# Softmax reciprocals in three bfloat16 parts, and counts as bfloat16 matmuls, in an attention and mixture-of-experts kernel

## The chip, the cores and the metric

The kernel runs on one core of one Trainium2 chip. A core has five engines with a queue of instructions each: TensorE (PE in the profile, with its weight loads as PEld), VectorE (DVE), ScalarE (ACT), GpSimd (POOL), and SyncE (SP), which here only issues DMA transfers. Every queue is worked off in order. The metric is the device time in microseconds of one execution.

## The reference, cut to what matters

One layer: attention with a gated relative position bias, a layer norm, a top-2 mixture of 8 experts with a capacity per expert, and a second layer norm. The input has 8 batches of 1024 tokens of width 256; there are 16 heads of width 16.

```python
scores = jnp.einsum('bhid,bhjd->bhij', q, k) * scale + gated_bias
attn = jax.nn.softmax(scores, axis=-1)
out = jnp.einsum('bhij,bhjd->bhid', attn, v)
...
x = _layernorm(x + out.transpose(0, 2, 1, 3).reshape(B, N, E) @ Wo.T + bo)
...
for e in range(E):                      # the experts, in order
    match = topk_experts == e
    elig = match.any(-1) & ~fallback
    pos = jnp.cumsum(elig) - 1          # a token's place in the expert's buffer
    kept = elig & (pos < cap)
    overflow = elig & (pos >= cap)
    ...
    fallback = fallback | overflow
```

Two things in it matter here: the softmax's division by a sum per row and head, and the running count of tokens per expert (`cumsum`), from which each token's place follows.

## The kernel before, in words

The kernel has two halves. In the first, attention runs and the tokens are sorted by expert into a DRAM buffer `xd`; in the second the experts run over that buffer. The change touches only the first half.

**Units and steps.** The first half is a loop over 64 *units* (8 batches by 8 pairs of heads, `HP = 2`), each of 16 *steps*: 8 blocks of 128 keys (`j`) by 2 chunks of 512 queries (`c`). The loop variable is `g`; `u, s = divmod(g, STEPS)`. The scheduler is switched off here: each engine gets its instructions in the order in which this loop calls the helpers. A step does this:

- `scores` (L1107): two bfloat16 matmuls into the PSUM tile `sc`; `exps` (L1120): DVE adds the gated bias `gb` near the diagonal, ACT writes `pr = exp(sc)`.
- `products` (L1137), in each odd step: `v` times `pr` into the PSUM tile `o_acc`, for four pairs of head and chunk at partitions 0, 32, 64 and 96. `v` has a 17th column of ones, so row `r + D` of each group of 32 holds the sums of the softmax.
- `max_first`, `max_second`, `max_fold`: 21 steps ahead of it (`LEAD`), the row maxima for a later unit: four matmuls into `pm` (L1028, L1032), a relu on ACT into `over` (L1057), a fold on DVE (L1069). `shift` (from step 11) turns the maxima of a unit into two rows of `qs`.
- POOL makes `gb` two blocks ahead (`gate_biases`, L988) and the diagonal matrices `dgb` (L1001).
- SP issues the loads for later units in fixed steps: `biasb` (step 1), `ks` and its differences (3 and 4), `qs` (6), two halves of `gates` (8 and 15), `bias` (0).

**The division, before.** At the end of step 1 of unit u+1, `take_outputs(u)` (L1151) lets ACT copy `o_acc` to `osb`. What follows is put into a list of deferred calls by `after(n, what)`; `tick`, once in a step, counts down and calls what is due. One step on, four DMAs spread the four rows of 512 sums over 128 partitions by 16 columns (`move_sums`, L1159). Two steps after that DVE takes the reciprocal (L1175), one step later four DMAs bring them back as four rows of 512, `recs` (L1169). In step `DIVIDE_AT = 10`, `divide` (L1178) is queued: a float32 matmul of the 4x128 matrix `sel` with `recs` spreads each row over 32 partitions (`pb`, L1182), DVE multiplies `osb` by it (L1186), and four DMAs store the result into `oD` (L1196). `osb` has one buffer, so the next unit's copy of `o_acc` waits for these stores.

**The shared bank.** One PSUM bank (`bank(name)`) serves all side work: the projections of the next batch (`prologue`), the output projection, the router and the counting of the batch before (`epilogue`), the shift and the division. `Streams` hands it out. A side task is a generator that yields what it needs: BANK (a matmul into the bank comes next), HELD or SLOW (the bank is read in the next step, by ACT or by DVE), FREE or ODD. While a task holds the bank nobody else gets it. `streams.own` has the shift and the division, which come first:

```python
if u and s == DIVIDE_AT:
    streams.own.append(divide(u - 1))
if s == SHIFT_AT and u + 1 < UNITS:        # SHIFT_AT = 11
    streams.own.append(shift(u + 1))
behind = c == 0 and streams.read == SLOW
others = s + 1 != SHIFT_AT
if not behind:
    streams.bank(others)
```

**The counts, before.** In the epilogue, for each of the eight experts and the fallback, POOL makes running sums within a partition (`running`, L812; its operations all carry the line L754) into `prefix` and `incl`. `count` (L822) then makes two float32 matmuls with constant 128x128 matrices: `ones` against the batch's running sums (L824), and `later` against the batch's own marks (L825), both into `pc`. DVE reads `pc` and gives the place and the spill, from which POOL goes on with the next expert. In the last batch these nine counts run after the loop, with nothing beside them. The epilogue then starts `scatters`, which sends one indirect store from POOL (L891) in each odd step.

Of the kernel before, what the change touches and what calls it, by code (L numbers as in the profile page):

```python
# [11 lines left out]
F32 = mybir.dt.float32  # L12
BF16 = mybir.dt.bfloat16
# [3 lines left out]
ALU = mybir.AluOpType  # L17
# [4 lines left out]
P = 128  # L22
H, D = 16, 16
NG, HG = 4, 4
E = H * D
NE, TOP_K = 8, 2
FF = 1024
NBUCKET, MAX_DIST = 80, 200
CH = 512
# [14 lines left out]
HP = 2  # L44
LEAD = 21
SHIFT_AT = -LEAD % 16
DIVIDE_AT = 10
EPS = 1e-5


# [28 lines left out]
def tile_attention_moe(  # L79
# [25 lines left out]
    nc = tc.nc  # L105
    B, N, _ = x.shape
    T = B * N
    NI = N // P
# [44 lines left out]
    with ExitStack() as at:  # L153
        cst = at.enter_context(tc.tile_pool(name="cst", bufs=1))
# [3 lines left out]
        rt = at.enter_context(tc.tile_pool(name="rt", bufs=1))  # L158
# [24 lines left out]
        def load_piece(b, n, tag="xp", bufs=3):  # L183
# [21 lines left out]
            out=gb_ld.rearrange("p g o -> p (g o)"), in_=gru_b.to_broadcast([P, 8])  # L205
# [59 lines left out]
        for base, sign in ((0, 1), (D - 1, -1)):  # L265
# [17 lines left out]
            out=later, in_=later, compare_op=ALU.is_gt, fill=0.0, base=0,  # L283
            pattern=[[-1, P]], channel_multiplier=1,
        )
        sel = cst.tile([4, 4, 32], F32, name="sel")
        nc.gpsimd.memset(sel, 0.0)
        nc.gpsimd.affine_select(
            out=sel, in_=sel, compare_op=ALU.not_equal, fill=1.0, base=0,
            pattern=[[-1, 4], [0, 32]], channel_multiplier=1,  # L290
        )
        rank = cst.tile([P, NE], F32, name="rank")
        nc.gpsimd.iota(
            rank, pattern=[[-1, NE]], base=NE, channel_multiplier=0,
# [27 lines left out]
        for lo, hi in zip(cuts[:-1], cuts[1:]):  # L322
# [9 lines left out]
            out=blocks,  # L332
# [48 lines left out]
        for h in range(HP):  # L381
# [2 lines left out]
                nc.sync.dma_start(out=pattern[r : r + NI, h, :], in_=kcr[:NI, :])  # L384
            for r in range(R_SHIFT, R_ALL):
                nc.sync.dma_start(out=pattern[r : r + 1, h, :], in_=kcr[8:9, :])
        incl = [cst.tile([P, NE + 1, NI], F32, name=f"incl{i}") for i in range(2)]
        prefix = [cst.tile([P, 2 * NI], F32, name=f"prefix{i}") for i in range(3)]
        for t in prefix:
            nc.vector.memset(t, 0.0)  # L390
        o_acc = ps_o.tile([P, CH], F32, name="o_acc")
# [55 lines left out]
        def after(n, what):  # L447

            waiting.append([n, what])
# [230 lines left out]
        def epilogue(b, me):  # L680
# [140 lines left out]

            def count(e):  # L822
                pc = bank("pc")[:, :NI]
                nc.tensor.matmul(pc, ones, now[:, e, :], start=True, stop=False)  # L824
                nc.tensor.matmul(pc, later, who, start=False, stop=True)  # L825
                return pc

            spill = small("spill", NI)
# [26 lines left out]
            if b == B - 1:  # L855
                yield BANK
                pf = bank("pf")[:, : NE + 1]
                nc.tensor.matmul(pf, ones, now[:, :, NI - 1], start=True, stop=True)
                yield SLOW
                nc.vector.tensor_copy(counts, pf)  # L860
            ts = slice(b * NI, (b + 1) * NI)
# [289 lines left out]
        def take_outputs(u):  # L1151
            me = units[u]
            me.osb = work.tile([P, CH], F32, tag="osb", name=f"osb{u}", bufs=1)
            nc.scalar.copy(me.osb, o_acc)

            def move_sums():
                me.sums = rt.tile([P, 4 * CH // P], F32, tag="sums", name=f"sums{u}")
                for r in range(4):
                    nc.sync.dma_start(  # L1159
                        out=me.sums[r * 32 : (r + 1) * 32, :],  # L1160
                        in_=me.osb[r * 32 + D : r * 32 + D + 1, :].rearrange(
                            "o (p n) -> o p n", p=32
                        ),
                    )

            def move_back():
                me.recs = rt.tile([4, CH], F32, tag="recs", name=f"recs{u}")
                for r in range(4):
                    nc.sync.dma_start(  # L1169
                        out=me.recs[r : r + 1, :].rearrange("o (p n) -> o p n", p=32),  # L1170
                        in_=me.sums[r * 32 : (r + 1) * 32, :],
                    )

            after(1, move_sums)
            after(3, lambda: nc.vector.reciprocal(me.sums, me.sums))  # L1175
            after(4, move_back)

        def divide(u):  # L1178
            b, hp = divmod(u, UB)
# [140 lines left out]
                yield FREE  # L1320
                yield from prologue(b + 1, pieces)

        for g in range(G + 12):
            u, s = divmod(g, STEPS)
            j, c = divmod(s, NCH)
            b, sb = divmod(g, UB * STEPS)
# [323 lines left out]
```

## Time and profile before

| what | value |
|---|---|
| median of 3 runs | 3645.89 us (3643.89 to 3651.33) |
| the profiled execution: time, span | 3639.7 us, 3638.0 us |
| granted TensorE clock, mean | 0.962 |
| PE, DVE, ACT, POOL busy | 90%, 53%, 56%, 61% of the span |
| relu of the maxima on ACT (L1057), 1024 times | 597 ns each |
| exp on ACT (L1134), 1024 times | 1024 ns each |
| gated bias on POOL (L988), 512 times | 2092 ns each in the mean |
| the divide's matmul (L1182), 128 records for 64 divides | 646 ns each |
| reciprocal on DVE (L1175), 128x16, 64 times | 244 ns each |
| DMA issues of sums and of recs on SP, 256 each | 0.58 and 0.59 us each (median) |

How to read it: the profile is one execution. Busy shares are averages over both halves. A float32 matmul shows as two records, a bfloat16 one as one record with its load. The span counts from the first to the last instruction, and the measured time has a little around it. An idle time ahead of an instruction is put down to what ended it, the *releaser*. The time of a transfer's issue is SP's own; the data land later.

### The profile page before, as it was taken

How to read it: one execution, taken by the hardware profiler on the slowest of the kernel's cores; microseconds unless marked ns; L12 is line 12 of the kernel's file. 1: busy time of each engine (PE TensorE's matmuls, PEld its weight loads, DVE VectorE, ACT ScalarE, POOL GpSimd, SP SyncE). 2: the span in 40 equal slices, each digit the busy share in tenths (PEclk: the TensorE clock that was granted, in tenths of full speed). 3: DMA queues.
4: the chain of work that ended last, by engine and by line, in shares of the span. 5: the costliest groups of instructions: out<-in, count | busy, mean ns of one | idle time of the engine just before them, and what ended most of it. 6: DMA issues, size and time to landing. Idle time of an engine off the chain costs nothing. (4 is left out here: it accounts for less than half of the span.)

```text
span 3638.0 us, 53431 instructions
## 1 busy us (share of the span) xinstructions
PE 3266.2 (90%) x16263; PEld 1651.2 (45%) x16263; DVE 1926.7 (53%) x5559; ACT 2043.5 (56%) x3084; POOL 2225.2 (61%) x2619
## 2 busy tenths in 40 slices
PE   4798999989999999999999999993399999999997
PEld 2332343334334334334334433332267677667776
DVE  2565656655765766665666576651134344444343
ACT  1676777767777777787777777771122222222222
POOL 3567667776886887787797688782233333333332
PEclk7998999999999999999999999995699999999999
DMA  6567766656643453444444444320332332232220
GB/s 167 150 177 190 190 169 179 198 164 179 190 138 112 145 157 113 135 141 128 143 124 137 126 139 141 116 95 14 113 84 58 88 89 67 88 94 88 72 91 21
DMA packets 380417, 455.70 MB, mean 125 GB/s; under 512 B 87477, under 2 KB 285234, under 8 KB 380106
## 3 DMA queue, kind: packets, MB, share of 16 engines
q1 hardware_dynamic: 339146, 388.06, 36.2%
q0 software_dynamic: 19296, 43.38, 4.2%
q10 hardware_dynamic: 21664, 20.58, 1.8%
q8 instruction: 138, 2.26, 0.3%
q14 instruction: 173, 1.42, 0.1%
HBM read 315.16 MB, written 140.54 MB: 125 GB/s over the span
## 5 line engine op out<-in xcount | busy, mean ns | idle before, releaser
L1134 ACT ACTIVATE pr<-sc 128x1024 f32<-128x1024 f32 x1024 | 1047.6, 1024 | 316.4 <-DVE sc L1127 297.1
L988 POOL TENSOR_TENSOR gb<-bias,gates 128x1024 f32<-128x1024 f32 (+2 forms) x512 | 1070.9, 2092 | 132.4 <-DMA gates<-gd 80.2
L1069 DVE CUSTOM_DVE_ANT_0 over<-pm,over 128x512 f32<-128x512 f32 x1024 | 704.0, 688 | 816.4 <-ACT over L1057 301.1
L1057 ACT ACTIVATE over<-pm 128x512 f32<-128x512 f32 x1024 | 611.4, 597 | 276.0 <-PE pm L1032 259.4
L1112 PE MATMUL sc<-qs,ks 122*128 122x512 bf16 x2048 | 618.6, 383 | 32.5 <-ACT pr L1134 19.3
L1127 DVE TENSOR_TENSOR sc<-sc,gb 128x640 f32<-128x640 f32 (+3 forms) x768 | 600.0, 781 | 79.9 <-POOL gb L988 62.6
L1032 PE MATMUL pm<-biasb,dgb 128*128 128x320 bf16 (+2 forms) x2048 | 578.5, 282 | 0.0
L1142 PE MATMUL o_acc<-pr,v 128*17 128x512 f32 x4096 | 553.9, 612 | 0.2 <-ACT pr L1134 0.2
L1488 PE MATMUL ph<-xsT,w 128*128 128x512 f32 (+1 forms) x1440 | 488.3, 497 | 13.0 <-ACT xsT L1428 12.1
L1503 PE MATMUL py<-w,hT 128*128 128x256 f32 x2208 | 485.0, 379 | 5.6 <-DVE ys L1510 5.6
L1503 PEld LDWEIGHTS py<-w,hT 128*128 128x128 f32 x2208 | 419.2, 190 | 74.3 <-issue 9.8
L1028 PEld LDWEIGHTS <-qs 120*128 120x128 bf16 x2048 | 207.2, 101 | 518.4 <-issue 349.2
L1028 PE MATMUL pm<-ks_d,qs 120*128 120x512 bf16 x1024 | 392.8, 384 | 54.5 <-DMA qs<-qd 27.4
L1028 PE MATMUL pm<-ks,qs 120*128 120x512 bf16 x1024 | 396.7, 387 | 44.6 <-DVE mh L1069 26.4
L1495 ACT ACTIVATE hT<-ph,b_sb 128x512 f32<-128x512 f32 (+1 forms) x360 | 211.6, 588 | 288.0 <-PE ph L1488 259.9
L1488 PEld LDWEIGHTS ph<-xsT,w 128*128 128x128 f32 x1440 | 270.5, 190 | 213.1 <-issue 169.2
L1428 ACT COPY xsT<-pt 128x512 f32<-128x512 f32 (+1 forms) x90 | 39.5, 489 | 567.5 <-PE pt L1425 472.6
L143 POOL TENSOR_TENSOR rs<-rstd,neghalf 128x1 f32<-128x1 f32 x138 | 78.4, 568 | 441.3 <-DVE rstd L141 440.9
L1032 PEld LDWEIGHTS <-dgb 128*128 128x128 bf16 x2048 | 201.7, 98 | 260.6 <-issue 147.4
L1001 POOL TENSOR_TENSOR dgb<-anti,grev 128x256 bf16<-128x256 f32 x512 | 314.5, 615 | 4.9
L1112 PEld LDWEIGHTS <-ks 122*128 122x128 bf16 x2048 | 198.0, 99 | 216.4 <-issue 67.7
L1523 POOL DMA_INDIRECT out_dram<-o,dst_i x138 | 145.4, 1054 | 154.3 <-DVE o L145 71.4
(184 smaller groups left out, 2840.9 us busy)
## 6 DMA issues: line engine op xcount, KB each, us to landing
gates<-gd SPq DMA_DIRECT2D x128, 704.0 KB
biasb<-stripb SPq DMA_DIRECT2D x128, 288.0 KB
bias<-blocks SPq DMA_DIRECT2D x64, 512.0 KB
xd<-zero SPq DMA_DIRECT2D x51, 522.0 KB
ks<-kd SPq DMA_DIRECT2D x384, 64.0 KB
qs<-qd SPq DMA_DIRECT2D x384, 64.0 KB
yd<-zero SPq DMA_DIRECT2D x40, 512.0 KB
w<-in_w_dram ACTq DMA_DIRECT2D x16, 1024.0 KB
```

Of the source, the lines that this page charges most:

```text
L988: nc.gpsimd.tensor_tensor(gb_[:, :, off : off + hi - lo], me.bias[:, :, off : off + hi - lo], gates[:, :, lo - at : hi - at], ALU.mult,)
L1001: nc.gpsimd.tensor_tensor(dg, anti.unsqueeze(1).to_broadcast([P, HP, P]), batches[b].grev[:, i, hp * HP : (hp + 1) * HP] .unsqueeze(2) .to ...
L1028: nc.tensor.matmul(pm, QS[u % 3][:R_SHIFT, h, i * P : (i + 1) * P], keys, start=True, stop=False)
L1032: nc.tensor.matmul(pm[:, lo:hi, :], dgb[m - h][:, h, :], me.biasb[:, at : at + (hi - lo) * P].rearrange("p (j n) -> p j n", n=P)[:, :, :HALF],
L1057: nc.scalar.activation(me.over, pm, AF.Relu)
L1069: nc.vector.tensor_tensor_reduce(out=me.over, in0=me.rest, in1=me.over, scale=1.0, scalar=-3.0e38, op0=ALU.add, op1=ALU.max, accum_out=me. ...
L1112: nc.tensor.matmul(me.sc[:, h, :], ks[:, h, j * P : (j + 1) * P], qs[:, h, c * CH : (c + 1) * CH], start=True, stop=True,)
L1127: nc.vector.tensor_tensor(sc[:, :, lo - c * CH : hi - c * CH], sc[:, :, lo - c * CH : hi - c * CH], me.gb[j][:, :, off : off + hi - lo], A ...
L1134: nc.scalar.activation(pr, sc, AF.Exp)
L1142: nc.tensor.matmul(o_acc[r : r + D + 1, :], batches[b].v[:, j, hp * HP + h, :], prs[c][:, h, :], start=(j == 0), stop=(j == NI - 1),)
L1488: nc.tensor.matmul(ph[:, :size], w1_sb[:, k, f * P : (f + 1) * P], xsT[:, k, :size], start=(k == 0), stop=(k == NK - 1),)
L1503: nc.tensor.matmul(py, hT[:, f, t * P : (t + 1) * P], w2_sb[:, f, :], start=(f == 0), stop=(f == NF - 1),)
```

## The change

The sums go to 96 partitions by 64 columns instead of 128 by 16. Three DMAs put the same 4 rows of 512 sums on partitions 32 to 63, 64 to 95 and 96 to 127 of one tile `sums`, whose first 32 partitions hold ones. DVE takes the reciprocal of the whole tile, in the same step as before. Then a float32 reciprocal is written as the sum of three bfloat16 numbers: ACT rounds all partitions to bfloat16 into `rp`, and POOL subtracts what was rounded from the partitions 64 up (`first`, step 5); ACT rounds what remains on these, and POOL leaves on the partitions 96 up what then remains (`others`, step 6). So `rp[32:64]`, `rp[64:96]` and `rp[96:]` are the first, second and third part. In step 9 one DMA brings the 96 partitions back as 12 rows of 512. The divide is queued in step 12 and multiplies them by a 12x128 matrix `sel` in bfloat16, which adds the three parts up.

The tiles of the counts and the two constant matrices become bfloat16; whole numbers up to 256 are exact in it, and the counts that enter the matmuls are at most 64.

```diff
-DIVIDE_AT = 10
+DIVIDE_AT = 12
...
-        sel = cst.tile([4, 4, 32], F32, name="sel")
+        sums = cst.tile([P, 4 * CH // 32], F32, name="sums")
+        nc.vector.memset(sums[:32], 1.0)
+        ones16 = cst.tile([P, P], BF16, name="ones16")
+        nc.gpsimd.tensor_copy(ones16, ones)
+        later16 = cst.tile([P, P], BF16, name="later16")
+        nc.gpsimd.tensor_copy(later16, later)
+        sel = cst.tile([12, 4, 32], BF16, name="sel")
         nc.gpsimd.memset(sel, 0.0)
-        nc.gpsimd.affine_select(
-            out=sel, in_=sel, compare_op=ALU.not_equal, fill=1.0, base=0,
-            pattern=[[-1, 4], [0, 32]], channel_multiplier=1,
-        )
+        for a in range(3):
+            nc.gpsimd.affine_select(
+                out=sel, in_=sel, compare_op=ALU.not_equal, fill=1.0, base=-4 * a,
+                pattern=[[-1, 4], [0, 32]], channel_multiplier=1,
+            )
...
-        incl = [cst.tile([P, NE + 1, NI], F32, name=f"incl{i}") for i in range(2)]
-        prefix = [cst.tile([P, 2 * NI], F32, name=f"prefix{i}") for i in range(3)]
+        incl = [cst.tile([P, NE + 1, NI], BF16, name=f"incl{i}") for i in range(2)]
+        prefix = [cst.tile([P, 2 * NI], BF16, name=f"prefix{i}") for i in range(3)]
...
-                nc.tensor.matmul(pc, ones, now[:, e, :], start=True, stop=False)
-                nc.tensor.matmul(pc, later, who, start=False, stop=True)
+                nc.tensor.matmul(pc, ones16, now[:, e, :], start=True, stop=False)
+                nc.tensor.matmul(pc, later16, who, start=False, stop=True)
...
             def move_sums():
-                me.sums = rt.tile([P, 4 * CH // P], F32, tag="sums", name=f"sums{u}")
-                for r in range(4):
+                for a in range(3):
                     nc.sync.dma_start(
-                        out=me.sums[r * 32 : (r + 1) * 32, :],
-                        in_=me.osb[r * 32 + D : r * 32 + D + 1, :].rearrange(
-                            "o (p n) -> o p n", p=32
-                        ),
+                        out=sums[(a + 1) * 32 : (a + 2) * 32, :],
+                        in_=me.osb[D::32, :].rearrange("r (p n) -> r p n", p=8),
                     )
+
+            def first():
+                me.rp = rt.tile([P, 4 * CH // 32], BF16, tag="rp", name=f"rp{u}")
+                nc.scalar.copy(me.rp, sums)
+                nc.gpsimd.tensor_tensor(sums[64:], sums[64:], me.rp[64:], ALU.subtract)
+
+            def others():
+                nc.scalar.copy(me.rp[64:], sums[64:])
+                nc.gpsimd.tensor_tensor(me.rp[96:], sums[96:], me.rp[96:], ALU.subtract)
 
             def move_back():
-                me.recs = rt.tile([4, CH], F32, tag="recs", name=f"recs{u}")
-                for r in range(4):
-                    nc.sync.dma_start(
-                        out=me.recs[r : r + 1, :].rearrange("o (p n) -> o p n", p=32),
-                        in_=me.sums[r * 32 : (r + 1) * 32, :],
-                    )
+                me.recs = rt.tile([12, CH], BF16, tag="recs", name=f"recs{u}")
+                nc.sync.dma_start(
+                    out=me.recs.rearrange("q (p n) -> q p n", p=8), in_=me.rp[32:]
+                )
 
             after(1, move_sums)
-            after(3, lambda: nc.vector.reciprocal(me.sums, me.sums))
-            after(4, move_back)
+            after(3, lambda: nc.vector.reciprocal(sums, sums))
+            after(4, first)
+            after(5, others)
+            after(8, move_back)
...
-        for g in range(G + 12):
+        for g in range(G + DIVIDE_AT + 2):
```

The matmul that counts the totals after the last batch (L858) takes `ones16` in the same way.

## The prediction

> **What bounds the kernel now.** I read the page's first two parts, then the busy time by stretch, the waits of PE, the groups by line and shape, and the timeline around one divide.
>
> ```profile
> PE 3266.2 (90%) x16263; PEld 1651.2 (45%) x16263; DVE 1926.7 (53%) x5559; ACT 2043.5 (56%) x3084; POOL 2225.2 (61%) x2619
> ...
> PE   4798999989999999999999999993399999999997
> ...
> PEclk7998999999999999999999999995699999999999
> ```
>
> PE is full in both halves except at the start and at the seam (slices 27 and 28), where it idles and its granted clock falls. The change lies wholly in the first half (attention, to about 2545 us). The second half is not touched. By stretch, columns as in the header:
>
> ```profile
> core 0: us, PE busy (x) PEld busy (x) DVE busy (x) ACT busy (x) POOL busy (x), PEclk, DMA share, GB/s
> 1584.10:1613.90 29.80, 28.52 (x165) 9.94 (x164) 20.08 (x47) 24.75 (x35) 27.03 (x25) 1.00 0.54 158
> 1107.40:1149.30 41.90, 37.77 (x207) 15.66 (x205) 23.93 (x54) 31.53 (x52) 30.98 (x34) 1.00 0.42 117
> ```
>
> The first is a bare unit of 16 steps, the second one that also carries projections. In both PE leads: 1.3 us of 29.8 idle, 4.1 of 41.9. ACT has 5.1 and 10.4 us to spare, POOL only 2.8 and 10.9. So what leaves PE shortens a unit, until POOL stands in the way. PE's own waits:
>
> ```profile
> PE pm L1028 <- DMA qs<-qd: 27.4, 16, 8.0
> PE pm L1028 <- DVE mh L1069: 26.4, 56, 1.7
> PE sc L1112 <- ACT pr L1134: 19.3, 22, 5.1
> ...
> PE pb L1182 <- DMA recs<-sums: 11.7, 4, 9.1
> ```
>
> The first is a queue effect; the timeline shows where it arises (start, duration, engine):
>
> ```profile
> 1009.46 2.44 SPq L1169 DMA_DIRECT2D recs<-sums  x4
> ...
> 1012.54 2.67 SPq L918 DMA_DIRECT2D qs<-qd  x6
> ...
> 1013.45 1.09 PE L1182 MATMUL pb<-recs,sel 4*128 4x512 f32 x2
> ...
> 1014.47 0.39 PE L1028 MATMUL pm<-ks,qs 120*128 120x512 bf16 x1
> ...
> 1017.26 0.38 PE L1028 MATMUL pm<-ks_d,qs 120*128 120x512 bf16 x1 [1.88 <-DMA qs<-qd]
> ```
>
> SP spends 2.44 us on issuing the four recs loads, then the six qs loads for the unit after next; PE needs those at step 11 and stands 1.88 us. And pb holds PE from 1013.45 to 1014.47, 1.02 us.
>
> **The change part by part.**
>
> *The divide's matmul.* The groups by line and shape (busy, mean ns, idle before):
>
> ```profile
> L1182 PE MATMUL pb<-recs,sel 4*128 4x512 f32 x128 | 72.5, 646 | 21.3 <-DMA recs<-sums 11.7 <-DVE dif L654 5.2 <-DVE mh L1069 3.1
> ...
> L825 PE MATMUL pc<-prefix,later 128*128 128x8 f32 x144 | 28.3, 269 | 0.0
> L824 PE MATMUL pc<-incl,ones 128*128 128x8 f32 x144 | 27.1, 260 | 29.0 <-POOL incl L754 29.0
> ...
> L1175 DVE RECIPROCAL sums<-sums 128x16 f32<-128x16 f32 x64 | 15.6, 244 | 12.8 <-DMA sums<-osb 12.6
> ```
>
> A float32 matmul is two records, so a divide costs 72.5/64 = 1.13 us of PE. With bfloat16 it is one record of 512 columns; the nearest row is the scores matmul sc (122x512 bf16, 383 ns mean). Twelve rows instead of four stream no longer. Gain 64 x (1.13 - 0.38) = 48 us, all on the engine that bounds. Slots in the timeline give about 50: 1.02 us against some 0.22 from one bfloat16 512-column matmul to the next.
>
> *The counts.* 72 counts of two float32 matmuls, each two loads (about 190 ns) and two records. Two counts stand in the timeline beside scores: from pc's first record to the next matmul 0.47 us (934.30 to 934.77) and 0.36 us (939.55 to 939.91). With bfloat16 two loads of 98 to 101 ns (rows L1032, L1028) and two short records remain. Bounds: 0.20 us per count if the loads are not hidden, 0.10 if they are. No 8-column bfloat16 row exists; I take 0.2, nearer the two loads. 63 counts x 0.22 = 14 us. The last nine run alone at the seam in a chain of 3.03 us each, of which PE holds 1.06 (2514.39 to the DVE's 2515.45); half of it saved gives 9 x 0.5 = 4 us. POOL's small operations take 200 ns in float32; output in bfloat16 is no dearer (L422, 128x512 to bf16, 1158 ns, against L675, to float32, 1181). Together 18 us.
>
> *SP's queue.* Before, eight issues per unit (4 sums, 4 recs, 0.58 us each in the table of tiles); after, three and one. The recs load also moves from step 5, ahead of qs<-qd, to step 9, behind it and the gates load. So qs<-qd goes out 0.6 + 2.44 = 3.0 us earlier. Of its 27.4 us of waits 8.0 belong to unit 0, which has no divide. The other 15 waits (19.4 us, 2.0 us at most) should go. What is late next is the second row of the waits (DVE's fold), so I count 15. The gates load also goes out earlier, which POOL waits for but PE does not.
>
> The moved recs load has its own deadline. By the order of instructions the divide does not run at step 12 but at 13: at step 12 the shift still holds the shared bank. From issue at 9 that is four steps, 7.5 us at 29.8/16 = 1.86 us each. Ahead of it lies the gates load, 704 KB, at 158 GB/s 4.6 us. The Trainium skill (DMA: Bandwidth & Descriptors, Queues, rings and completion order) says that an engine of the DMA consumes descriptors in ring order, which speaks against this place: 96 small packets wait for the whole 704 KB. With the rule recs land some 6 us after the gates issue, some 3 us ahead of the divide (gates is issued at step 8); if they overtook it, more. Neither makes PE wait, so nothing is charged; but a unit with other traffic could lose a microsecond.
>
> *Later stores.* The product on DVE moves from step 11 to 14, the four oD stores with it, and since they stand on SP ahead of gates, bias and biasb of the next unit, those slip by about 3 us (SP today waits 271.9 us for that product at L1196, so SP has the room). Then the next sums load queues behind 704 + 512 + 2 x 288 KB. In a bare unit the reciprocal, four steps into the next unit, may wait for it: 0 at best, 1 us in some 35 bare units at worst. DVE is 67% busy there and passes only part on to PE: I charge 10 us, and keep 0 to 35. osb itself is overwritten at the next unit's step 1, three steps after the stores: 5.6 us for 4 issues of 0.58 and the landing; tight but enough.
>
> *DVE.* The reciprocal grows from 16 to 64 columns. Rows: 203 ns at 8 columns (L768), 244 at 16, so 5.1 ns per column and 490 ns at 64. The Trainium skill (VectorE: DVE Perf Modes, First, the fixed hardware budget) gives an iterative divide with a repeat count of 8; eight cycles of its 0.96 GHz are 8.3 ns per column, estimated 644 ns. By the rows DVE gains 64 x 0.25 = 16 us of work, by the rule 26. I take the rows. It hides under DVE's third of idle time.
>
> *ACT and POOL.* Two copies on ACT per unit: 128x16 takes 173, 128x256 405, so 128x64 about 0.25 us, 32 us in all; ACT keeps over 4 us of room per bare unit. Two subtractions on POOL: 128x64 takes 321 ns (L754), so 0.64 us per unit, 41 in all. POOL has room except in the last and first unit of a batch, where each odd step also sends an indirect store of 1.01 us. There DVE waits for POOL today (62.6 us in 43 waits, DVE sc L1127 <- POOL gb L988), so 8 units pay 0.64: 5 us. Those units also don't cash the 1 us saved on PE: 8 us.
>
> The wait that is added: ACT's second copy (step 6) stands behind POOL's first subtraction (step 5), and behind ACT's copy stand relu and exp, for which PE waits. Where POOL is on time the chain is copy, subtract, copy inside one step. Where it lags, in those two units per batch, ACT can stand up to about 3 us: in the unit that starts at 1026.0 POOL ends step 5's dgb at 1047.1, ACT ends step 6's exp at about 1044.4. Mostly this takes the place of DVE's wait for gb further on; I charge 1 us in 8 units, 8 us; bounds 0 and 16 x 3 = 48.
>
> *The rest.* Three constants, two copies and two selects at the start, beside the first loads: nothing; if that cover were gone, 1 us. The tail trades four issues against two copies and two subtractions: 0, within 1.5 us either way.
>
> **The sum.** 48 + 18 + 15 - 10 - 5 - 8 - 8 = 50 us. It is made against the profiled execution, 3639.7 us (span 3638.0 and 1.7 around it), which gives 3590. The runs shown have their median 6 us above it, 3645.9; there the same gain gives 3596. I predict 3592 between them.
>
> **The rivals.**
> 1. *PE takes it all.* Slack hides every added piece, and the qs waits go entirely: 48 + 18 + 19 = 85, with 50 for the divide 87, about 3558. For it: PE leads in nearly every unit. Against: POOL's 2.8 us of room. Chance 0.25.
> 2. *POOL or ACT stands next.* The stalls at step 6 and the late sums cost their upper bounds in part, some 50 to 60 us instead of 31: gain 15 to 30, about 3622. For it: the 62.6 us that DVE waits for POOL today. Chance 0.18.
> 3. *Slower.* One place: the reciprocal behind the next unit's loads. If the ring is not drained by step 4, DVE, and behind it the fold and every score, stand in each unit. The gross gain of 81 is eaten from 1.3 us per unit (81/64); at 2 us per unit it costs 128 against 81 and the time is about 3690. For it: the loads slip by 3 us and DVE already waits for sums (12.6 us, six times). Against: units with projections are 36 to 46 us long and have room; only bare ones are tight. Chance 0.09.
> 4. *No change in sum*, within 0.2% (7 us, about what a measurement of this kernel can tell): 0.04, between 2 and 3.
> The forecast case, 3570 to 3610, has 0.44.
>
> The range: 3550 leaves out about half of rival 1's tail, 3635 takes in rival 2; some 0.2 lie outside. Faster: 0.44 + 0.25 + 0.18 = 0.87; same 0.04; slower 0.09.
>
> **What would show it.** Right: pb one record of about 0.38 us per divide and 25 us in all; PE pm <- qs<-qd down to unit 0's 8 us; the bare unit 28.5 to 29 us instead of 29.8; the second half unchanged. Wrong: a row of DVE sums <- DMA sums<-osb above 50 us (rival 3); a row of ACT's copy into rp waiting for POOL above 30 us (rival 2); PE pb <- DMA recs in many units (the moved load too late); ACT's copy of o_acc waiting for the oD stores.

## The result and the profile after

The changed kernel takes 3737.81 us (median of 4 runs, 3734.93 to 3739.59), against 3644.89 us of the kernel before (3638.43 to 3651.33): a ratio of 1.0254, 95% interval 1.0235 to 1.0274. It is 93 us slower; the forecast was 50 us faster.

The page of the profiled execution (span 3735.5 us):

```profile
PE 3258.7 (87%) x16054; PEld 1625.1 (44%) x16054; DVE 1948.7 (52%) x5560; ACT 2064.3 (55%) x3212; POOL 2259.9 (60%) x2751
...
PE   4898898889889889898988988985199999999998
...
PEclk7999899999999999999999999996599999999999
```

PE executes 209 records fewer (two of float32 became one in 64 divides, four became two in 72 counts, two one in the last count), yet its busy time falls by only 7.5 us, and 9s have become 8s over the whole first half. The mean granted clock is 0.949 instead of 0.962. The second half runs as before. From the first score matmul to the end of the last, before and then after (length, PE busy with its records, granted clock, DMA):

```profile
117.48:2456.03 2338.55, 2176.79 (x12001) 0.98 0.51 150
```

```profile
119.96:2552.15 2432.19, 2167.97 (x11811) 0.96 0.49 144
```

94 of the 97.5 us by which the two spans differ lie there. PE's busy time in these units fell by 9 us, and its idle time grew by 102.

The groups by line and shape (busy, mean ns, idle before) show that each changed operation has about the size that was forecast:

```profile
L1199 PE MATMUL pb<-recs,sel 12*128 12x512 bf16 x64 | 25.0, 391 | 17.9 <-DMA recs<-rp 17.8
L834 PE MATMUL pc<-incl,ones 128*128 128x8 bf16 x72 | 12.4, 173 | 75.5 <-POOL incl L764 67.8 <-DVE mh L1079 6.0
L1190 DVE RECIPROCAL sums<-sums 128x64 f32<-128x64 f32 x64 | 34.9, 545 | 40.3 <-DMA sums<-osb 40.2
L1177 POOL TENSOR_TENSOR sums<-sums,rp 64x64 f32<-64x64 f32 x64 | 19.4, 304 | 185.6 <-ACT rp L1176 102.8 <-ACT lg L755 19.9 <-DMA ks_d<-dd 14.4
L1180 ACT CAST rp<-sums 64x64 bf16<-64x64 f32 x64 | 15.4, 241 | 31.4 <-POOL sums L1177 30.1
```

What is not as forecast is the last column. POOL now stands 102.8 us for ACT's first copy, a wait that the kernel before does not have. Its running sums for the counts (`incl`) come late for PE; that this follows from the tie to ACT is shown by two of the experiments (`e7` and `e8`). PE's waits:

```profile
PE pc L834 <- POOL incl L764: 67.8, 28, 7.7
PE sc L1122 <- ACT pr L1144: 41.4, 40, 3.6
PE pm L1038 <- ACT over L1067: 39.0, 58, 4.3
PE pm L1038 <- DVE mh L1079: 36.5, 73, 2.9
PE pb L1199 <- DMA recs<-rp: 17.8, 2, 16.9
PE po L698 <- DMA oD<-osb: 16.2, 8, 2.5
...
PE pm L1038 <- DMA qs<-qd: 9.8, 3, 6.1
```

Before, the first two were 29.0 and 19.3 us, the third and the wait of the output projection for `oD`

```profile
PE pm L1028 <- ACT over L1057: 6.7, 18, 0.9
PE po L688 <- DMA oD<-osb: 1.8, 2, 1.4
```

These four rows grew by 108 us together; the wait for `qs` went from 27.4 to 9.8, as forecast.

Where does it come from within a batch? The stretches of a unit with nothing beside it, of a batch's first unit and of its sixth:

```profile
core 0: us, PE busy (x) PEld busy (x) DVE busy (x) ACT busy (x) POOL busy (x), PEclk, DMA share, GB/s
1635.90:1665.40 29.50, 28.07 (x164) 9.86 (x162) 20.82 (x49) 25.02 (x37) 24.67 (x32) 1.00 0.48 148
1354.40:1396.50 42.10, 34.07 (x173) 11.49 (x171) 21.42 (x48) 25.09 (x37) 35.19 (x32) 0.92 0.43 138
1568.00:1603.50 35.50, 30.36 (x171) 10.37 (x170) 21.11 (x57) 25.19 (x37) 25.98 (x49) 0.90 0.35 108
```

The bare unit did get shorter (29.8 before), though not to the 28.5 to 29 that were to show the forecast right. The first unit, 32.4 us before, takes 42.1, the sixth 35.5 instead of 31.0. Over the eight batches the first units lost 64 us together and the sixth units 28. In that first unit the timeline shows the mechanism (start, duration, engine, in brackets the idle time before and its releaser):

```profile
1363.09 1.01 POOL L901 DMA_INDIRECT xd<-xt,slot_i  x1 [2.73 <-DMA xd<-xt,slot_i]
...
1364.12 2.37 POOL L998 TENSOR_TENSOR gb<-bias,gates 128x1024 f32<-128x1024 f32 x1
...
1366.53 1.10 DVE L1137 TENSOR_TENSOR sc<-sc,gb 128x896 f32<-128x896 f32 x1 [3.27 <-POOL gb L998]
...
1367.72 1.02 ACT L1144 ACTIVATE pr<-sc 128x1024 f32<-128x1024 f32 x1 [3.78 <-DVE sc L1137]
...
1368.80 0.59 PE L1122 MATMUL sc<-qs,ks 122*128 122x512 bf16 x2 [2.85 <-ACT pr L1144]
...
1371.70 1.91 PE L1152 MATMUL o_acc<-pr,v 128*17 128x512 f32 x8
...
1375.63 0.30 POOL L1177 TENSOR_TENSOR sums<-sums,rp 64x64 f32<-64x64 f32 x1 [0.31 <-POOL dgb L1011]
1375.97 0.24 ACT L1180 CAST rp<-sums 64x64 bf16<-64x64 f32 x1 [3.35 <-POOL sums L1177]
```

In the same unit of the kernel before:

```profile
1326.98 1.01 POOL L891 DMA_INDIRECT xd<-xt,slot_i  x1 [2.31 <-DMA xd<-xt,slot_i]
...
1330.42 1.10 DVE L1127 TENSOR_TENSOR sc<-sc,gb 128x896 f32<-128x896 f32 x1 [0.81 <-POOL gb L988]
```

POOL has come to this unit with less lead: the store that waits for the one before it (2.73 us now, 2.31 then) begins 8.7 us after the start of the unit, 5.5 before. Now `gb` is late, VectorE stands 3.27 us, ACT 3.78, PE 2.85. Later POOL reaches its first subtraction, due in step 5, when the others are in step 8; ACT's second copy waits 3.35 us for it, and behind that copy stands the relu that PE waits for. And there is a second price. PE's busy time and granted clock around its stop:

```profile
core 0: us, PE busy (x), PEclk, DMA share, GB/s
1365.90:1368.80 2.90, 0.05 (x2) 1.00 0.38 101
1368.80:1370.20 1.40, 1.36 (x6) 1.00 0.81 236
1370.20:1374.00 3.80, 3.80 (x14) 0.55 0.77 251
```

In the 3.8 us that begin 1.4 us after a stop of 2.85 us the mean clock is 0.55; the eight `o_acc` records take 1.91 us instead of 1.05 earlier in the same unit. So this wait of PE cost itself and, a moment later, more in slow matmuls: 3.8 x 0.45 = 1.7 us on top of 2.85. Not every wait does (see the clock, below).

### The profile page after: what moved, and what is told of

It is laid out like the page before. It is cut to its first block, busy times and chain, and to the rows that moved or that the text cites. A ratio compares the mean times of both kernels' runs of the same rounds, so it can differ in the third digit from the quotient of the medians.

```text
span 3735.5 us, 52631 instructions
## 1 busy us (share of the span) xinstructions
PE 3258.7 (87%) x16054; PEld 1625.1 (44%) x16054; DVE 1948.7 (52%) x5560; ACT 2064.3 (55%) x3212; POOL 2259.9 (60%) x2751
## 5 line engine op out<-in xcount | busy, mean ns | idle before, releaser
L998 POOL TENSOR_TENSOR gb<-bias,gates 128x1024 f32<-128x1024 f32 (+2 forms) x512 | 1070.1, 2090 | 42.1 <-DMA gates<-gd 19.7
L1122 PE MATMUL sc<-qs,ks 122*128 122x512 bf16 x2048 | 633.4, 391 | 44.4 <-ACT pr L1144 41.4
L1042 PE MATMUL pm<-biasb,dgb 128*128 128x320 bf16 (+2 forms) x2048 | 587.2, 287 | 2.2 <-POOL biasb L957 2.2
L1152 PE MATMUL o_acc<-pr,v 128*17 128x512 f32 x4096 | 561.5, 620 | 0.2 <-ACT pr L1144 0.2
L1038 PE MATMUL pm<-ks_d,qs 120*128 120x512 bf16 x1024 | 400.3, 391 | 66.4 <-ACT over L1067 39.0
```

Source lines behind the costliest of these rows:

```text
L998: nc.gpsimd.tensor_tensor(gb_[:, :, off : off + hi - lo], me.bias[:, :, off : off + hi - lo], gates[:, :, lo - at : hi - at], ALU.mult,)
L1038: nc.tensor.matmul(pm, QS[u % 3][:R_SHIFT, h, i * P : (i + 1) * P], keys, start=True, stop=False)
L1042: nc.tensor.matmul(pm[:, lo:hi, :], dgb[m - h][:, h, :], me.biasb[:, at : at + (hi - lo) * P].rearrange("p (j n) -> p j n", n=P)[:, :, :HALF],
L1122: nc.tensor.matmul(me.sc[:, h, :], ks[:, h, j * P : (j + 1) * P], qs[:, h, c * CH : (c + 1) * CH], start=True, stop=True,)
L1152: nc.tensor.matmul(o_acc[r : r + D + 1, :], batches[b].v[:, j, hp * HP + h, :], prs[c][:, h, :], start=(j == 0), stop=(j == NI - 1),)
```

## The experiments

Times stand against the kernel before, run beside them; "+" is slower, and us are differences of medians within a comparison.

**The two matmul terms alone.** `e1_counts_only` has only the bfloat16 counts of the change; `e10_pb_only` has a one-part bfloat16 divide and nothing else (parts two and three are left out):

```diff
-        sel = cst.tile([4, 4, 32], F32, name="sel")
+        sel = cst.tile([4, 4, 32], BF16, name="sel")
...
-            after(3, lambda: nc.vector.reciprocal(me.sums, me.sums))
+            after(3, invert)       # reciprocal of me.sums into me.rp, BF16; recs BF16
```

> The kernel before with the counts alone in bfloat16 (ones16, later16, incl, prefix); the division stays as it was. Theory A (the handshake: GpSimd, tied to ScalarE's two copies at steps 5 and 6, loses its lead, and what lies behind it comes late) and theory B (the late divide: the bank handed out three steps later shifts the side work, and the oD stores come late for the output projection) both expect the prediction's term for the counts, 14 to 22 us faster, about 3627, since neither touches this part. If it is slower, bfloat16 counts are themselves a cause.

> The kernel before with the divide's matmul in bfloat16 with one part: VectorE's reciprocal writes bfloat16, the 4x128 matrix and recs are bfloat16; the second and third parts are left out, so nothing is added on ACT or POOL and no step moves. It shows what the term 'divide matmul' (48 us in the prediction) is worth by itself. If PE sets the pace of the units, 3645 - 45 to 50, about 3597. If PE's shorter work is mostly taken by waits for the maxima (ACT, VectorE) and for POOL, 3620 to 3640.

Counts alone: -10 us (ratio 0.9980, 0.9962 to 0.9997). The one-part divide alone: -11 us (0.9968, 0.9956 to 0.9981), of a saving of PE that was 48 us. PE's busy time did fall, to 3231.7, by 34.5. What took it, in the waits of PE in `e10_pb_only`:

```profile
PE pm L1028 <- DMA qs<-qd: 47.1, 24, 7.9
PE pm L1028 <- DVE mh L1069: 30.8, 60, 1.9
```

Instead of 27.4 and 26.4: PE only arrives earlier at loads that have not landed. In 5 of the 24 waits for `qs` SP had not even issued the load when PE stopped.

**The divide two steps later.** `e2_late_only`:

```diff
-DIVIDE_AT = 10
+DIVIDE_AT = 12
...
-        for g in range(G + 12):
+        for g in range(G + DIVIDE_AT + 2):
```

> The kernel before with DIVIDE_AT = 12 (and two more closing steps), nothing else: float32 sums, four recs loads at step 5. Theory A: no handshake, so only the 2 us per batch that TensorE waits for oD, about 3645 to 3665. Theory B: most of the loss is here, 3700 to 3740 (the after kernel's 92 us, and the 60 us that its lighter matmuls save can be hidden under it).

+80 us (1.0226, 1.0204 to 1.0249). Two numbers cost nearly the whole loss of the change, with no operation added. The wait for `oD` at the output projection is there (15.3 us, 1.8 before), and VectorE's fold (44.7, 26.4 before) and `qs` (49.0, 27.4 before) make PE wait longer. The wait for `incl` is not: 27.7 us, 29.0 before.

**The copies and subtractions.** On the kernel before, the change's four operations on scratch tiles in steps 5 and 6: once as a chain that depends like the change's (`e7`), once without any dependence (`e8`), and the two subtractions alone (`e11`):

```diff
+            def first():
+                me.hp = rt.tile([P, 64], BF16, tag="hp", name=f"hp{u}")
+                nc.scalar.copy(me.hp, hs)                       # e8: ha, hs;  e11: left out
+                nc.gpsimd.tensor_tensor(hs[64:], hs[64:], me.hp[64:], ALU.subtract)  # e8, e11: gs_, ga
+            def others():
+                nc.scalar.copy(me.hp[64:], hs[64:])             # e8: ha, hs;  e11: left out
+                nc.gpsimd.tensor_tensor(me.hp[96:], hs[96:], me.hp[96:], ALU.subtract)  # e8, e11: gb_o, gs_, ga
+            after(4, first)
+            after(5, others)
```

> The kernel before, with two copies on ScalarE and two subtractions on GpSimd added in steps 5 and 6 on scratch tiles, in the same chain (copy, subtract, copy, subtract, each waiting for the one before); nothing else reads the result. Theory of the handshake: 40 to 110 us slower (the run with early divide was 55 slower, and its matmuls save something like 50). Rival, that they cost only their own time on engines with room: within 10 us of before.

> The same four operations in the same places, but on separate scratch tiles, so that no copy waits for a subtraction and no subtraction for a copy; nothing reads the results. Theory of the handshake: within 15 us of before. Rival, that the engines' time itself costs (GpSimd is 90% busy in a bare unit): as slow as the run with the chain.

> The kernel before with the two subtractions on POOL alone (0.3 us each, on scratch tiles, in steps 5 and 6 of each unit), without the two ACT copies. With both engines' operations and no dependence the cost was 49 us. If POOL's time is what costs (41 us of POOL work in 64 units, POOL being the engine that runs with little slack between a batch's count and gated bias), this alone costs 35 to 50: 3680 to 3695. If ACT's copies delay exp and relu on the chain to PE, this costs under 15: 3645 to 3660.

The chain: +104 us (1.0283, 1.0258 to 1.0307). Without dependence: +49 (1.0125, 1.0101 to 1.0149). The subtractions alone: +61 (1.0164, 1.0150 to 1.0179). So 0.6 us more on POOL per unit, 41 us in all, costs more than itself, and the dependence about as much again. The copies on ACT cost nothing that shows; that `e11`, without them, was a little slower than `e8`, with them, is not explained (the two stand in different comparisons). The same first unit of a batch in the kernel before, and then in `e11_pool_only` (columns as above):

```profile
1321.50:1353.90 32.40, 31.28 (x173) 11.44 (x171) 20.70 (x48) 24.13 (x34) 28.62 (x25) 1.00 0.54 162
```

```profile
1337.40:1378.20 40.80, 33.84 (x173) 12.09 (x171) 20.77 (x48) 24.37 (x34) 32.70 (x31) 0.92 0.46 138
```

The loss has a place: in the traces the first and fifth units of the batches and the very last unit carry 53 of the 60 us by which the units grew. In units 6 to 8 of a batch POOL was already busy some 27 of 30 us; the reading is that what is added there is paid in the next batch's first unit. PE's 173 records took 2.6 us longer at the lower clock, and over the whole run PE's busy time rose by 31.5 us with no matmul added: about half of the 61 us. The chain's own signature in `e7_handshake_only`:

```profile
POOL hs L1183 <- ACT hp L1182: 89.0, 26, 11.4
...
POOL gb L990 <- DMA gates<-gd: 22.8, 7, 6.5
...
ACT hp L1186 <- POOL hs L1183: 34.2, 14, 6.6
```

In the kernel before:

```profile
POOL gb L988 <- DMA gates<-gd: 80.2, 21, 11.6
```

A wait for `gates` is lead: POOL stands ready before its data are there. In the chain it waits for ACT instead, and most of the lead is gone. PE's wait for the counts in `e7`, and then in `e8`, with the same operations and no dependence:

```profile
PE pc L826 <- POOL incl L756: 59.4, 25, 7.7
```

```profile
PE pc L832 <- POOL incl L762: 28.2, 11, 7.7
```

So the late `incl` of the change is the chain's, and its wait for `oD` (1.4 us in `e7`, 15.3 in `e2`) the late divide's.

**The change without its parts.** Four runs change the changed kernel: `e3` puts the divide back at 10 (and the load of the reciprocals two steps earlier), `e4` puts the four part operations on VectorE, `e5` does both, and `e6` does them all in one step with the reciprocal:

```diff
-DIVIDE_AT = 12
+DIVIDE_AT = 10                                   # e3, e5, e6
...
-                nc.scalar.copy(me.rp, sums)
-                nc.gpsimd.tensor_tensor(sums[64:], sums[64:], me.rp[64:], ALU.subtract)
+                nc.vector.tensor_copy(me.rp, sums)       # e4, e5, e6; others() likewise
+                nc.vector.tensor_tensor(sums[64:], sums[64:], me.rp[64:], ALU.subtract)
...
-            after(8, move_back)
+            after(6, move_back)                  # e3, e5;  e6: after(4, ...)
```

> The changed kernel with DIVIDE_AT = 10 as before and the recs load at step 7 instead of 9 (after(6, move_back)); the three parts by ScalarE and GpSimd and the bfloat16 counts stay. Theory A: the handshake is whole, so the loss stays, 3690 to 3740. Theory B: the loss goes and the savings show, 3570 to 3620. Between them: both have a share.

> The changed kernel with all four operations on the parts (two copies, two subtractions) on VectorE in the same steps 5 and 6; ScalarE and GpSimd have none of them; the divide stays at step 12. Theory A: GpSimd keeps its lead, 3570 to 3630. Theory B: the loss stays, 3700 to 3740.

> The changed kernel with both suspects taken out: DIVIDE_AT = 10, the recs load at step 7, and the four operations on the parts on VectorE in steps 5 and 6. Joint theory (the two costs are separate and hide the same saving: late divide alone +80 us, parts on ScalarE and GpSimd at the old divide +55): the saving shows, 3570 to 3620. If a third cost remains (the sums or recs load too late, the bfloat16 matmuls themselves), it stays above 3640.

> As the run with early divide and parts on VectorE, but all five operations (reciprocal, two copies, two subtractions) back to back in step 4 and the recs load at step 5, ahead of the qs loads, as in the kernel before. Joint theory: 3575 to 3625, with VectorE held for about 1.3 us in one piece in each unit, of which TensorE may see up to half (0 to 40 us). A rival, that VectorE is already the next bound, expects it 30 us or more above the run that spreads them over three steps.

`e3` +55 us (1.0161, 1.0141 to 1.0181), `e4` +66 (1.0194, 1.0167 to 1.0221), `e5` +15 (1.0043, 1.0023 to 1.0063), `e6` +37 (1.0104, 1.0083 to 1.0125). Undoing one of the two costs gives back 38 or 27 us, undoing both 78. What is left in `e5` points to VectorE: PE waits 64.2 us for its fold (26.4 before), and the four operations take 3.1 us per unit in the mean, where their shortest durations make 0.8. In its trace (ns: least, median, most):

```profile
L1176 DVE CAST rp<-sums x64: 182/207/3137, 170.2 to 2492.5; 128x64 bf16<-128x64 f32 x64
L1177 DVE TENSOR_TENSOR sums<-sums,rp x64: 222/561/3170, 170.4 to 2492.8; 64x64 f32<-64x64 f32 x64
L1180 DVE CAST rp<-sums x64: 192/1141/2826, 174.0 to 2493.0; 64x64 bf16<-64x64 f32 x64
```

A copy that can take 182 ns takes up to 3137. The next experiments came upon the reason.

**SP's issues.** `e9_one_dma` has the bfloat16 counts and the old float32 division at the old steps, with one DMA where there were four:

```diff
-                for r in range(4):
...
+                nc.sync.dma_start(
+                    out=me.sums, in_=me.osb[D::32, :].rearrange("r (p n) -> r p n", p=32)
+                )
...
-                for r in range(4):
...
+                nc.sync.dma_start(
+                    out=me.recs.rearrange("q (p n) -> q p n", p=32), in_=me.sums
+                )
```

> The counts as bfloat16 matmuls, the float32 division at its old steps (10), with one DMA for the sums and one for the reciprocals in place of four and four. It tests the SP term of the prediction (15 us for 6 of 8 issues and fewer waits of the maxima for qs). If the waits for qs are SP's issues, PE's wait for qs falls from 34 us (counts alone) to below 10 and the time is 3634 - 15 to 20, 3615 to 3620. If the waits only change places, as the other runs suggest, it is 3625 to 3640. Unlike the change, nothing here takes ACT or POOL time.

-53 us, 3588.57 us (0.9851, 0.9837 to 0.9865), 43 more than counts alone. One issue of all four rows takes 0.62 us (sums) or 0.64 (reciprocals), one of a single row 0.58 or 0.59, so SP saves 3.4 us per unit. How much of the 43 us is SP's time and how much comes of fewer and larger transfers was not taken apart. PE's wait for `qs`, 34.1 us with counts alone, is in `e9_one_dma`:

```profile
PE pm L1032 <- DMA qs<-qd: 7.8, 1, 7.8
```

**PE's saving on top of that.** `e14_one_part` is `e9_one_dma` with the one-part divide of `e10`. `e12_two_parts` makes two parts on VectorE from the 128x16 reciprocals, without the third; `e13_two_recips` replaces the copy in it by a second reciprocal:

```diff
+            def parts():
+                me.rp = rt.tile([P, 2, 4 * CH // P], BF16, tag="rp", name=f"rp{u}")
+                nc.vector.reciprocal(me.sums, me.sums)
+                nc.vector.tensor_copy(me.rp[:, 0, :], me.sums)   # e13: reciprocal(me.rp[:, 0, :], me.sums), put first
+                nc.vector.tensor_tensor(me.rp[:, 1, :], me.sums, me.rp[:, 0, :], ALU.subtract)
```

> The version with single DMAs and bfloat16 counts, and one bfloat16 part only (the second and third are left out): the reciprocal writes bfloat16, no operation is added anywhere. On the kernel before this saved 10 of 48 us. If SP's queue took the rest (PE's wait for qs rose from 27 to 47 us there), it saves 35 to 48 here: 3541 to 3554. If POOL's and VectorE's share of the units takes it, 5 to 15: 3574 to 3584.

> A version that may beat both: counts in bfloat16, one DMA for the sums, reciprocal in 128x16 as before, then two bfloat16 parts by two more VectorE operations on 128x16 (about 0.15 to 0.2 us each) in the same step, one DMA for each part (8 rows), bfloat16 divide matmul at the old step 10; nothing on ACT and POOL, and the third part is left out. If PE's saving of about 60 us can be had once no engine is loaded and no step is moved: 3575 to 3600. If VectorE's extra 25 us at that place costs one for one and PE's time is worth half: 3620 to 3640.

> The two-part version once more (third part left out), with VectorE's copy to bfloat16 (174 ns at least, 1350 ns in the mean) replaced by a second reciprocal that writes bfloat16. If that copy was held up beside POOL's work and cost the 40 us by which two parts were slower than single DMAs alone, VectorE's operations are 245 + 245 + about 180 ns, and the time is 3589 - 48 + 20 to 30, 3560 to 3575. If any 0.4 us more on VectorE at this step costs it, 3600 to 3630.

`e14_one_part`: -78 us, 3563.72 us (0.9785, 0.9768 to 0.9802), the fastest run of the study, though it leaves two parts out. Here the divide's shorter matmul is worth 25 of 48 us. Two parts: -13 us (0.9957, 0.9942 to 0.9972), so against one part two operations that take 174 ns at least, and one more DMA issue, cost 65 together. With a second reciprocal instead of the copy: -28 (0.9914, 0.9895 to 0.9933). In `e12_two_parts` the copy, and the subtraction after it, took

```profile
L1170 DVE CAST rp<-sums x64: 174/638/6150, 168.8 to 2458.7; 128x16 bf16<-128x16 f32 x64
L1171 DVE TENSOR_TENSOR rp<-sums,rp x64: 174/176/596, 169.0 to 2458.9; 128x16 bf16<-128x16 f32 x64
```

and with the copy gone, in `e13_two_recips`, it is the subtraction that is slow, while the reciprocals are not:

```profile
L1170 DVE RECIPROCAL rp<-sums x64: 241/243/254, 166.4 to 2444.8; 128x16 bf16<-128x16 f32 x64
L1172 DVE TENSOR_TENSOR rp<-sums,rp x64: 174/533/6057, 167.0 to 2445.3; 128x16 bf16<-128x16 f32 x64
```

The timeline of `e12_two_parts` around one such copy:

```profile
1143.76 2.35 POOL L993 TENSOR_TENSOR gb<-bias,gates 128x1024 f32<-128x1024 f32 x1
1144.24 0.24 DVE L1169 RECIPROCAL sums<-sums 128x16 f32<-128x16 f32 x1
...
1144.52 1.87 DVE L1170 CAST rp<-sums 128x16 bf16<-128x16 f32 x1
```

The copy starts while POOL works on `gb` (to 1146.11) and ends 0.28 us after it. Ten of the eleven copies that began with no POOL instruction running took 174 to 176 ns. The reciprocal beside the same `gb` is not held up. The Trainium skill (SBUF — State Buffer, Who interferes with whom) says the same: a VectorE copy to another type, or an operation with two inputs in SBUF, can need the port pair that GpSimd uses, and whichever comes second waits for the whole instruction of the other. The first part of it is what `e12` shows, the second what `e13` shows. But the wait can outlast one instruction: the copy of 6150 ns, which began at 754.21 us, lasted through five POOL instructions after the one that it began beside and ended at POOL's next pause.

**The two costs again, on the faster base.** `e15_one_dma_late` is `e9` with `DIVIDE_AT = 12`, `e16_one_dma_pool` is `e9` with the two subtractions of `e11`:

> The version with single DMAs and bfloat16 counts, with the divide two steps later (12) and nothing else. On the kernel before this alone cost 80 us. If it costs through the order of work in the bank (shift ahead of the divide, counts and projections one step later, the output projection's wait for oD), it costs 60 to 85 here too: 3650 to 3675. If it costs through SP, whose stores of the division then stand ahead of the loads of gates and qs, the shorter queue takes most of it away: 3600 to 3625.

> The version with single DMAs and bfloat16 counts, with the two subtractions on POOL (scratch tiles, 0.3 us each, steps 5 and 6). On the kernel before they cost 61 us. If POOL's lead at the end of a batch is what they use up, they cost as much or more here, where the units are shorter: 3650 to 3665. If the cost came by SP's loads being late, under 25: below 3615.

Against `e9`: the late divide +52 us (its ratio to before is 0.9996, 0.9986 to 1.0006), the subtractions +72 (1.0046, 1.0032 to 1.0060). So neither comes by SP's queue alone; of the late divide's 80 us some 30 are gone with the shorter queue. In `e15` PE's waits grew against `e9` for `oD` by 16 us, for the fold by 13, for the relu by 11, and its busy time by 14. The first of these:

```profile
PE po L692 <- DMA oD<-osb: 17.9, 8, 2.6
```

It is 2 us in each of eight batches: the epilogue begins 14 steps into a batch, and the division of the last unit before it, now in step 13, has not landed. Besides, the order of work in the bank has moved: the traces of `e15` and of the change show the counts, and most of the projections, one step later than `e9` and the kernel before. Which of these moves costs what, in the waits for the fold and the relu, was not taken apart.

**Loosening the chain in the change itself.** `e17_spread` gives the second copy and subtraction to step 8 and the load to step 10; `e18_spread_early` to steps 7 and 8, with the divide at 10:

```diff
-            after(5, others)
-            after(8, move_back)
+            after(7, others)          # e18: after(6, others)
+            after(9, move_back)       # e18: after(7, move_back)
```

> The change with its second copy and subtraction three steps after the first (step 8 instead of 6) and the reciprocals' load one step later. ACT then reaches the second copy when POOL has long done its first subtraction. If ACT's wait for POOL inside one step (30 us shown as such, and what follows from it on relu, exp and PE) is what the chain costs, this gives 30 to 55 us back: 3683 to 3708. If it is the time on POOL that costs, wherever it stands, under 10: 3728 to 3738.

> The change with the divide back at step 10, the second copy and subtraction two steps after the first (step 7), the load in step 8. With them at steps 5 and 6 and the load in step 7 this was 3699. If the chain costs: 3650 to 3670. If POOL's time costs: 3690 to 3700, and then also the reciprocals may come late for the divide, which PE would show as a wait for recs.

`e17`: +72 us (1.0209, 1.0182 to 1.0236), 20 us less than the change; below the 30 expected of the chain, above the 10 of mere time. PE's wait for the relu falls from 39.0 to 27.8 us, but POOL still waits 81.0 us for ACT's first copy, and the later load has a price of its own: PE waits 38.0 us for the reciprocals (17.8 in the change). `e18`: +63 (1.0174, 1.0152 to 1.0195), no better than `e3`. Its waits for `incl` and the relu are shorter than in `e3` (48.2 against 61.0 us, 26.2 against 36.3), but that for the reciprocals, 22.0 us there, is as its expectation named:

```profile
PE pb L1199 <- DMA recs<-rp: 93.9, 29, 7.9
```

Later parts with an early divide bring the reciprocals too late. Of the places tried, none is both loose and in time.

## Why the prediction was wrong, point by point

What failed is the pricing of what the change adds. The sum charged 31 us for it: 10 for the later stores and 21 for ACT and POOL, as if each piece cost its own time in a few units. Measured alone, the late divide costs 80 us and the chain of copies and subtractions 104. What failed beside it is the premise that what leaves PE shortens a unit: the two matmul terms, 66 us in the sum, were worth 21.

- *The divide's matmul*, 48 us of PE: the record came at 391 ns and with the float32 version of the same base (`e9` to `e14`) PE's busy time fell by 51 us. That twelve rows take no longer than four was right too (391 ns, 383 in `e14`). Right as work, wrong as time: 11 us on the kernel before, 25 with SP's queue short.
- *The counts*, 18 us: PE's busy time fell by 22, the time by 10 (1 to 14 by the interval).
- *SP's queue*, 15 us: the waits for `qs` fell by 17.6, as forecast. The same lever can be worth more: in `e9` six issues less per unit gave 43 us, more than all of the matmuls.
- *"So what leaves PE shortens a unit, until POOL stands in the way"*: the premise failed first. A bare unit's 1.3 us of idle PE was read as PE's lead over all else. The engines hand each step on to each other in order; PE, 90% busy, arrived earlier at the others' results when it alone got faster (`e10`: PE's busy time 34.5 us less, the time 11).
- *Later stores*, charged 10 us, kept to 0 to 35: measured at 80 alone and 52 on the faster base. The prediction followed the sums' load, whose row did rise (12.6 to 40.2 us of VectorE's waits), and did not follow the bank: the output projection's wait for `oD`, and the step by which counts and projections slip.
- *ACT and POOL*, 5 + 8 + 8 us: measured at 104 for the chain, and at 49 to 61 for its operations without the dependence. The step that failed is the room: "POOL has room except in the last and first unit of a batch". It has little: in units 6 to 8 it is busy some 27 of 30 us and lives on a lead, and what is taken from the lead is paid in the first. For ACT's wait within a step it kept "bounds 0 and 16 x 3 = 48"; the row shows 30.1 us; but POOL's wait for ACT, 102.8 + 80.4 us, is the other half of the same chain and was not counted. With it POOL's wait for `gates`, its lead, shrinks (80.2 to 22.8 us in `e7`).
- *The clock*: no term. `e14` and the changed kernel execute the same 16054 PE records, in 3185.0 and 3258.7 us of busy time, at clocks of 0.965 and 0.949. Of these 74 us (ends of matmuls are modelled, so as a size only) some 50 are the clock's. By the clock's records PE worked 160 us of the changed kernel's units at half clock, 83 in the kernel before and 58 in `e14`, and half of such time is lost. Another 14 came with the late divide alone (`e15` against `e9`) at no lower a clock. Nor does every wait bring the half clock on: in `e15` PE stood 42 us longer in the units than in `e9`, with 68 us of half clock in both.
- *VectorE's reciprocal*: 545 ns, between the 490 of the rows and the 644 of the page; the rows were nearer.
- *Recs in time*: right, PE waits for them only in the tail (16.9 of 17.8 us; 9.1 in the kernel before). From the last score to the end the two kernels differ by 1.4 us. The order in the ring, on which the deadline was reckoned, no run here shows by itself.
- *Rivals*: rival 3 had the sign, by a reciprocal behind the loads; its own mark, 50 us in VectorE's row, was not reached (40.2). Rival 2's was, narrowly: ACT's copy waits for POOL 30.1 us, over its 30. The rival's mechanism was right in part, its price several times too low, and the case that it stood for ends slower, not faster.

Single costs do not add up: late divide and chain alone make 184 us, the matmuls give back 21 and SP's shorter queue an amount that was not measured in the change's form; together it is 93. In part they fall in the same place: the first unit of the batch at 1354 us takes 42.1 us with both, 37.0 with the late divide alone, 41.3 with the chain alone, 32.4 with neither. Open are the bank order's share of the late divide beyond the wait for `oD`, why the subtractions without copies cost no less than with them, and how much of the chain's cost in the change is dependence: spreading it gave back 20 us, net of a longer wait for the reciprocals, of the 55 by which the chain on scratch tiles stood above the free operations.

## What to carry to other kernels

In a kernel whose engines pass each step on in order, the room of an engine is its lead at the tightest place, not its idle share: add up what it has to do in a row of units before the one where it is waited for, and count a dependence on another engine's queue as the loss of that lead. Before speeding up the busiest engine, look at what it will then wait for; here the plain merging of eight DMA issues into two was worth more than all bfloat16 matmuls, and made these worth more. Small pieces of work on VectorE beside long GpSimd instructions are to be priced by what they take there (1.35 us in the mean for the copy of `e12`), not by their least duration (0.17).

## What the runs showed of the hardware

- After PE stood 2.85 us, the mean granted clock was 0.55 over 3.8 us, beginning 1.4 us after work resumed. The Trainium skill (TensorE: Matmul & The Clock Gate, The HAM clock gate) tells of a window of about 3.4 us of idling that halves the clock; here a stop shorter than that was enough. In the changed kernel's trace the clock changes on a grid of 3.41 us. Between 170 and 2547 us each stretch of that grid at full clock with less than 1.48 us of PE busy was followed by one at half clock, none with more than 1.83, and in between it went both ways; no stretch had to be wholly idle. The bounds are those of this trace: in the kernel before, half clock also followed 2.67 us of busy time.
- A VectorE copy to bfloat16 of 128x16 took 174 ns alone and up to 6150 beside GpSimd, through several of its instructions in a row; a subtraction of two SBUF tiles 174 to 6057; a reciprocal of the same size 241 to 254 always.
- The reciprocal took 244 ns for 16 columns and 545 for 64: 6.3 ns for each further column.
- One DMA of four rows spread over 128 partitions took SP 0.62 to 0.64 us to issue, as against 0.58 to 0.59 for one of one row.
